# Seven half products with sums of halves for layer 1's scores, in place of eight

## The chip, the core and the metric

The program runs on one core of a Trainium2 chip. The metric is the device time of one execution in microseconds (us); the time of a kernel is the median of its runs. Engines are named as in the profile: PE (TensorE matmuls), PEld (TensorE weight loads), DVE (VectorE), ACT (ScalarE), POOL (GpSimd) and SP (SyncE, here an issuer of DMAs).

## The reference, cut to what matters

The input is 8 images of 256 channels and 32 x 32 positions, all in fp32. Layer 0 is attention with 8 heads. Layer 1 works on the tokens `t` (8 batches, 1024 tokens, 256 channels):

```python
t = t + attn(_ln_t(t), W)          # layer 1, attention
t = t + ffn(_ln_t(t), ...)         # layer 1, top 2 of 8 experts
...
xa = jnp.einsum('bnd,ed->bne', x, W)
scores = jnp.einsum('bne,bme->bnm', xa, x)
attn = jax.nn.softmax(scores, axis=-1)
y = jnp.einsum('bnm,bmd->bnd', attn, x)
```

The scores of a batch are a product of a 1024 x 256 matrix (`xa`) and a 256 x 1024 matrix (the normed tokens, turned). The softmax runs along each row, and its weights multiply the normed tokens.

## The kernel before, in words

One loop runs over the eight batches. In each, `layer0` computes layer 0's attention, `attend` layer 1's attention, and `normed` and `dispatch` the second norm, the gates of the experts and the scattering of tokens to them. Experts are worked for batches 0 to 6 together (`experts`) between layer 0 and `attend` of the last batch, and the last batch goes through all experts (`dense`). The results of the seven others are added up during `attend` and `dense` of the last batch, at the places where `tick` is called (class `Results`).

Engines take their instructions in the order in which they stand in that engine's queue. A scheduler has set that order from dependences and priorities; `issue_after` adds an edge for it alone. Work of the next batch is put in at the places where `attend` and `normed` call `fill`: class `Begin` issues the next batch's value products (`pv`, L399) and first projections (`pqk`, L340) there.

`attend` (L661 to L758) works on tiles of 128 tokens, so a batch has NT = 8 blocks. It normalises the tokens (`n1`), turns them to channels in `nT` (two halves of 128 channels, 1024 tokens each), and multiplies by W to get `xa` (`px`, L673, evicted by DVE at L680). For each block i, `scores(i)` makes four products of 128 x 512 (L688: two channel halves accumulate, for two halves of the tokens), DVE takes the maximum of the 1024 scores (L696), and ACT makes the exponentials with their sum (L699). The weights have then to be turned. For blocks 1 to 6, `turn` does it by a DVE transpose of squares of 32 (L706, into `sq`) and 16 moves of squares (L713, into `aT`), half by ACT copies and half by DMAs that SP issues. For blocks 0 and 7, `turn_now` uses TensorE transposes (L720) and one DVE copy (L722). `mix` multiplies the turned weights with the normed tokens (eight products of 128 x 256, L729), and DVE divides by the sum and adds the residual (L735). A block's mix stands two blocks behind its scores.

Exponentials, squares and turned weights come from one pool of six tiles (`expp`), which is also the pool of layer 0's exponentials (L520), and are taken in turn. PSUM has three tiles of two banks (`big`) and two of one bank (`acc`). The tiles of `two` named `qk0` and `qk1` hold layer 0's queries and keys, and in the last batch the hidden rows of `dense` and the results to store. The single tile `res` of `one` holds layer 0's result until its last product (L654), and in the last batch alternates with `v` as the home of the other batches' sums (`Results.load`).

Of the kernel before, what the change touches and what calls it, by code (L numbers as in the profile page):

```python
# [10 lines left out]
F32 = mybir.dt.float32  # L11
I32 = mybir.dt.int32
AF = mybir.ActivationFunctionType
# [6 lines left out]
def kernel(  # L20
# [49 lines left out]
    one = ctx.enter_context(tc.tile_pool(name="one", bufs=1))  # L70
    two = ctx.enter_context(tc.tile_pool(name="two", bufs=2))
    four = ctx.enter_context(tc.tile_pool(name="four", bufs=4))
    expp = ctx.enter_context(tc.tile_pool(name="expp", bufs=6))
    small = ctx.enter_context(tc.tile_pool(name="small", bufs=6))
    rowp = ctx.enter_context(tc.tile_pool(name="rowp", bufs=4))
    keep = ctx.enter_context(tc.tile_pool(name="keep", bufs=8))
    ps_big = ctx.enter_context(tc.tile_pool(name="ps_big", bufs=3, space=bass.MemoryType.PSUM))
    ps_acc = ctx.enter_context(tc.tile_pool(name="ps_acc", bufs=2, space=bass.MemoryType.PSUM))

    def big(name):  # L80

        return ps_big.tile([P, 1024], F32, tag="big", name=name)

    def acc(name):

        return ps_acc.tile([P, 512], F32, tag="acc", name=name)
# [146 lines left out]
    class Norm:  # L233


        def __init__(self, t, dst, eps, name):
            self.t, self.dst, self.eps, self.name = t, dst, eps, name
            self.mv = small.tile([P, NT, 2], F32, tag="mv", name=f"mv_{name}")
            self.rstd = small.tile([P, NT], F32, tag="rstd", name=f"rstd_{name}")
# [213 lines left out]
    def layer0(b, xT, begun, routing, xs):  # L453
# [61 lines left out]
        def soften(at, h):  # L515

            g, j = steps[at]
            if h == 0:
                sums[at] = small.tile([P, 2], F32, tag="sums", name=f"sums_{b}_{g}_{j}")
            ex = expp.tile([P, 1024], F32, tag="exps", name=f"ex_{b}_{g}_{j}_{h}")  # L520
            nc.scalar.activation(  # L521
                ex,
                pss.pop((at, h)),
                AF.Exp,
                bias=nmaxes.pop((at, h)),
                scale=1.0,
                accum_out=sums[at][:, h : h + 1],
            )
            exps[at, h] = ex
# [129 lines left out]


    def attend(b, t1, fill, tick=nothing):  # L661
        n1 = one.tile([P, NT, D], F32, tag="n", name=f"n1_{b}")
        layer_norm(t1, n1, 1e-5, f"a{b}")
        fill("norm 1")
        nT = one.tile([P, NCC, S], F32, tag="nT", name=f"nT_{b}")
        to_channels(n1, nT, f"n1_{b}")
        fill("normed 1")
        xa = one.tile([P, NCC, S], F32, tag="xa", name=f"xa_{b}")
        for ec in range(NCC):
            px = big(f"px_{b}_{ec}")  # L670
            for dc in range(NCC):
                for n in range(NH2):
                    nc.tensor.matmul(  # L673
                        px[:, ts(n, 512)],
                        WT[:, dc, ts(ec, P)],
                        nT[:, dc, ts(n, 512)],
                        start=(dc == 0),
                        stop=(dc == NCC - 1),
                    )
            tick(("xa", ec), nc.vector.tensor_copy(xa[:, ec, :], px))  # L680

        t2 = t1

        def scores(i):
            psc = big(f"ps1_{b}_{i}")
            for ec in range(NCC):
                for n in range(NH2):
                    nc.tensor.matmul(  # L688
                        psc[:, ts(n, 512)],
                        xa[:, ec, ts(i, P)],  # L690
                        nT[:, ec, ts(n, 512)],
                        start=(ec == 0),
                        stop=(ec == NCC - 1),
                    )
            nmax = small.tile([P, 1], F32, tag="nmax", name=f"nmax_{b}_{i}")
            tick(("max", i), nc.vector.tensor_reduce(nmax, psc, AX.X, ALU.max, negate=True))  # L696
            ex = expp.tile([P, 1024], F32, tag="exps", name=f"ex1_{b}_{i}")
            ssum = small.tile([P, 1], F32, tag="ssum", name=f"ssum_{b}_{i}")
            nc.scalar.activation(ex, psc, AF.Exp, bias=nmax, scale=1.0, accum_out=ssum)  # L699
            return ex, ssum  # L700

        def turn(i, ex):


            sq = expp.tile([P, S], F32, tag="exps", name=f"sq_{b}_{i}")
            nc.vector.transpose(sq, ex)  # L706
            aT = expp.tile([P, S], F32, tag="exps", name=f"aT_{b}_{i}")
            to = aT.rearrange("p (m a q) -> p a m q", a=NQ, q=SQ)
            since = sq.rearrange("p (m k q) -> p k m q", k=NQ, q=SQ)
            for a in range(NQ):  # L710
                for k in range(NQ):
                    move = nc.sync.dma_start if (a + k) % 2 else nc.scalar.copy
                    move(to[ts(k, SQ), a], since[ts(a, SQ), k])  # L713
            return [aT[:, ts(m, P)] for m in range(NT)]

        def turn_now(i, ex):

            pt = big(f"pa_{b}_{i}")
            for m in range(NT):
                nc.tensor.transpose(pt[:, ts(m, P)], ex[:, ts(m, P)], ident)  # L720
            aT = two.tile([P, S], F32, tag="tr", name=f"aT_{b}_{i}")
            nc.vector.tensor_copy(aT, pt)  # L722
            return [aT[:, ts(m, P)] for m in range(NT)]

        def mix(i, aT, ssum):
            ahead = fill("last products") if i == NT - 1 else None
            py = acc(f"py_{b}_{i}")
            for m in range(NT):
                nc.tensor.matmul(  # L729
                    py[:, :D], aT[m], n1[:, m, :], start=(m == 0), stop=(m == NT - 1)  # L730
                )
            rs = small.tile([P, 1], F32, tag="rs1", name=f"rs1_{b}_{i}")
            nc.vector.reciprocal(rs, ssum)
            with tc.issue_after(ahead.ins) if ahead else nullcontext():
                mixed = nc.vector.scalar_tensor_tensor(  # L735
                    t2[:, i, :], py[:, :D], rs, t1[:, i, :], ALU.mult, ALU.add
                )
            tick(("mixed", i), mixed)

        pending = []
        for i in range(NT):
            ex, ssum = scores(i)
            if 0 < i < NT - 1:
                ex = turn(i, ex)
            pending.append((i, ex, ssum))
            if i == 2:
                first, ex, ssum = pending.pop(0)
                mix(first, turn_now(first, ex), ssum)  # L750
            elif i > 2:
                mix(*pending.pop(0))
        fill("last weights")
        (last, ex, ssum) = pending.pop()
        ex = turn_now(last, ex)
        mix(*pending.pop())
        mix(last, ex, ssum)
        return t2  # L758


# [423 lines left out]
    class Results:  # L1184
# [67 lines left out]
        def add(self):  # L1252
            at = self.added
            if at == len(self.units):
                return
            assert at < self.sent
            self.added += 1
            b, i = self.units[at]
            n = at // NT
            gate = self.group.kept[b][0]  # L1260
            total = self.totals[n]
            for k in range(2):
                added = nc.vector.scalar_tensor_tensor(
                    total[:, i, :],
                    self.slot(at)[:, k, :],
                    gate[:, k, i : i + 1],
                    total[:, i, :],
                    ALU.mult,
                    ALU.add,
                )  # L1270
# [10 lines left out]
        def tick(self, place, behind=None):  # L1281
            added, sent, stored = self.PLACES.get(place, (0, 0, 0))
            if place == ("max", 0):
                self.scored = behind
            if added:
                with tc.issue_after(behind.ins):
                    for _ in range(added):
                        self.add()
            for _ in range(sent):
                self.gather(behind)  # L1290
            for _ in range(stored):
                if self.whole:
                    b, total, n = self.whole.pop(0)
                    store(b, total, n)
# [135 lines left out]
    for b in range(B):  # L1430
# [71 lines left out]
```

## Time and profile before

| what | value |
|---|---|
| median of 3 runs | 2321.36 us (2319.68 to 2324.47) |
| profiled execution, its own time | 2336.53 us |
| its span | 2333.8 us |
| mean granted TensorE clock | 0.992 |
| PE, L688 (scores of layer 1) | 228.5 us in 512 records |
| PE, L729 (mix of layer 1) | 234.3 us in 1024 records |
| ACT, L713 (turning copies) | 154.4 us in 384 copies |
| DVE, L696 (maxima) | 77.9 us in 64 |
| ACT, L699 (exponentials) | 71.3 us in 64 |

A row of the profile's groups has the line, the engine, the operation, output and inputs by the program's names, the shapes, the count, then the busy time in us and the mean of one in ns, and behind the second bar the idle time of the engine just before these instructions, with what ended most of it. An fp32 matmul leaves two records, so that 32 products a batch over eight batches are the 512 records of L688. The chain of waits is followed back from the last instruction; each piece of it is either work or a wait. The table of stretches gives, for each stretch, the busy time of every engine and the number of its instructions.

### The profile page before, as it was taken

The numbers are of one execution on the slowest core, as the hardware profiler recorded it, in microseconds if no ns is written. First come the engines' busy times: TensorE is split into PE (matmuls) and PEld (weight loads), VectorE is DVE, ScalarE is ACT, GpSimd is POOL, SyncE is SP. The second block draws the span as 40 slices with busy tenths as digits, with TensorE's granted clock in tenths as the row PEclk, the third lists the DMA queues.
The fourth block names the chain that finished last, engine by engine and source line by source line (L and its number), as shares of the span: only waits on it lengthen the run. The fifth ranks groups of instructions, "written<-read, shape, count | busy, mean of one in ns | idle before, by whom it ended". The sixth has DMA issues, their size and how long they took to land.

```text
span 2333.8 us, 37688 instructions
## 1 busy us (share of the span) xinstructions
PE 2276.1 (98%) x13123; PEld 1230.4 (53%) x13123; DVE 1528.1 (65%) x3757; ACT 1093.0 (47%) x1955; POOL 409.7 (18%) x392
## 2 busy tenths in 40 slices
PE   9999999999999999999999999999998999999698
PEld 3345534663456335633564356435643388886465
DVE  5775578557855785578657764777568756435755
ACT  3663466346634663556355645465545622223211
POOL 0000012000200020003000300020002134445563
PEclk9999999999999999999999999999999999999899
DMA  8995201020102010201020102000110247765574
GB/s 294 385 386 153 67 14 42 10 55 11 46 5 59 6 51 1 46 19 53 3 46 19 49 8 46 19 26 12 27 38 19 78 110 192 196 188 170 160 211 111
DMA packets 278756, 200.07 MB, mean 86 GB/s; under 512 B 189576, under 2 KB 232232, under 8 KB 276776
## 3 DMA queue, kind: packets, MB, share of 16 engines
q1 hardware_dynamic: 252472, 139.14, 21.2%
q0 software_dynamic: 25008, 58.01, 7.8%
q8 instruction: 104, 1.70, 0.3%
q10 hardware_dynamic: 1088, 0.52, 0.1%
q14 instruction: 84, 0.69, 0.1%
HBM read 108.88 MB, written 110.90 MB: 94 GB/s over the span
## 4 chain that ended last, share of the span: by engine, by line
PE 88%; DVE 4%; DMA 3%; issue 3%; ACT 1%; POOL 0%; another core or an unknown queue 0%; SPq 0%; DVEq 0%; ACTq 0%; POOLq 0%
PE po L557 19%; PE psc L480 18%; PE ps L688 9%; PE py L729 8%; PE pqk L362 7%; PE pr L654 5%; PE pv L399 4%; PE ph L1119 3%; PE pe L1145 3%; PE pdy L1392 3%; PE pdh L1368 2%; PE px L673 2%; PE pqk L340 2%; DMA y<-yb 1%; DVE n L254 1%
## 5 line engine op out<-in xcount | busy, mean ns | idle before, releaser
L521 ACT ACTIVATE ex<-psc,nmax 128x1024 f32<-128x1024 f32 x512 | 570.0, 1114 | 308.9 <-DVE scrap L504 222.9
L557 PE MATMUL po<-ex,vs 64*64 64x512 f32 x4096 | 569.3, 592 | 9.9 <-SPq L567 9.0
L480 PE MATMUL psc<-qk,qk 64*64 64x512 f32 x4096 | 574.1, 593 | 3.4 <-ACT ex L521 3.3
L504 DVE TENSOR_SCALAR_CACHE_REDUCE scrap<-psc,nmax 128x512 f32<-128x512 f32 x512 | 384.5, 751 | 163.4 <-PE psc L480 136.2
L495 DVE TENSOR_REDUCE nmax<-psc 128x1 f32<-128x512 f32 x512 | 350.8, 685 | 9.5 <-PE psc L480 9.5
L480 PEld LDWEIGHTS psc<-qk,qk 64*64 64x64 f32 x4096 | 179.1, 132 | 280.1 <-ACT ex L521 131.5
L557 PEld LDWEIGHTS po<-ex,vs 64*64 64x64 f32 x4096 | 173.9, 132 | 285.6 <-issue 84.3
L729 PE MATMUL py<-n,aT 128*128 128x256 f32 x1024 | 234.3, 383 | 4.4 <-DMA aT<-sq 4.4
L688 PE MATMUL ps<-nT,xa 128*128 128x512 f32 x512 | 228.5, 592 | 0.0
L729 PEld LDWEIGHTS py<-n,aT 128*128 128x128 f32 x1024 | 196.3, 192 | 54.8 <-issue 27.2
L933 POOL DMA_INDIRECT rows<-n,d_at x112 | 108.8, 972 | 661.2 <-DVE nmax L495 660.9
L713 ACT COPY aT<-sq 32x256 f32<-32x256 f32 x384 | 154.4, 402 | 80.0 <-DVE sq L706 52.4
L860 POOL TENSOR_TENSOR t<-t,n 128x2048 f32<-128x2048 f32 x8 | 36.3, 4533 | 878.2 <-DVE n L254 878.2
L362 PE MATMUL pqk<-xT,wqkv 128*128 128x512 f32 x384 | 171.2, 599 | 0.0
L688 PEld LDWEIGHTS ps<-nT,xa 128*128 128x128 f32 x512 | 96.6, 190 | 102.4 <-issue 95.1
L696 DVE TENSOR_REDUCE nmax<-ps 128x1 f32<-128x1024 f32 x64 | 77.9, 1217 | 84.9 <-PE ps L688 84.9
L327 ACT ACTIVATE qk<-pqk,b_qks 128x512 f32<-128x512 f32 x124 | 85.6, 690 | 94.2 <-PE pqk L362 77.1
L362 PEld LDWEIGHTS pqk<-xT,wqkv 128*128 128x128 f32 x384 | 71.0, 190 | 99.9 <-issue 76.8
L1241 POOL DMA_INDIRECT yk<-y,yat x112 | 110.2, 984 | 73.7 <-issue 34.0
L399 PE MATMUL pv<-wqkv,xT 128*128 128x512 f32 x256 | 120.6, 599 | 1.5 <-DVE v L407 1.0
L654 PE MATMUL pr<-wo,res 128*128 128x256 f32 x512 | 111.9, 379 | 0.0
L654 PEld LDWEIGHTS pr<-wo,res 128*128 128x128 f32 x512 | 97.2, 190 | 17.0 <-ACT res L576 3.2
(209 smaller groups left out, 2333.7 us busy)
## 6 DMA issues: line engine op xcount, KB each, us to landing
rows<-wb SPq DMA_DIRECT2D x7, 8192.0 KB
xr<-rows SPq DMA_DIRECT2D x252, 64.0 KB
y<-yb POOLq DMA_DIRECT2D x63, 256.0 KB
aT<-sq SPq DMA_DIRECT2D x384, 32.0 KB
xs<-in_x_dram SPq DMA_DIRECT2D x64, 128.0 KB
out_dram<-oT SPq DMA_DIRECT2D x60, 128.0 KB
xT<-in_x_dram SPq DMA_DIRECT2D x7, 1024.0 KB
sums<-t SPq DMA_DIRECT2D x7, 1024.0 KB
```

The lines of the kernel that those rows point to most:

```text
L362: mm = nc.tensor.matmul(pq[:, ts(n, 512)], wqkv[:, cc, t, ts(g, P)], xT[:, cc, ts(n, 512)], start=(cc == 0), stop=(cc == NCC - 1),)
L399: nc.tensor.matmul(pv, self.xT[:, cc, ts(i, P)], wqkv[:, cc, 2, :], start=(cc == 0), stop=(cc == NCC - 1),)
L480: mm = nc.tensor.matmul(pss[at, h][ts(c, DK), ts(n, 512)], k[r, j * P + c * DK : j * P + (c + 1) * DK], q[r, ts(n, 512)], start=True, stop ...
L495: firsts[at, h] = nc.vector.tensor_reduce(nmax, pss[at, h][:, ts(0, 512)], AX.X, ALU.max, negate=True)
L504: seconds[h] = nc.vector.tensor_scalar(scrap, pss[at, h][:, ts(1, 512)], -1.0, nmaxes[at, h], ALU.mult, ALU.min, accum_out=nmax,)
L521: nc.scalar.activation(ex, pss.pop((at, h)), AF.Exp, bias=nmaxes.pop((at, h)), scale=1.0, accum_out=sums[at][:, h : h + 1],)
L557: mm = nc.tensor.matmul(po[n][ts(h, DK), :], vss[at][keys, h, :], exps[at, h][keys, ts(n, 512)], start=(j == 0 and turn == 0), stop=(j == ...
L654: nc.tensor.matmul(pr[:, :C], res[:, g, ts(i, P)], wo[:, g, :], start=(g == 0), stop=(g == NPAIR - 1))
L688: nc.tensor.matmul(psc[:, ts(n, 512)], xa[:, ec, ts(i, P)], nT[:, ec, ts(n, 512)], start=(ec == 0), stop=(ec == NCC - 1),)
L713: move(to[ts(k, SQ), a], since[ts(a, SQ), k])
L729: nc.tensor.matmul(py[:, :D], aT[m], n1[:, m, :], start=(m == 0), stop=(m == NT - 1))
L1241: ins = nc.gpsimd.indirect_dma_start(out=self.slot(at)[:, k, :], out_offset=None, in_=self.group.y[:, :], in_offset=bass.IndirectOffsetOnAxis(
```

## The change

The score product of a batch is taken as a product of 2 x 2 matrices of halves: `xa` in halves of tokens (rows) and channels, the normed tokens in halves of channels and tokens. In place of eight half products it makes seven, in the form that shares sums (Winograd's form of Strassen's product). For this, four sums of halves of `nT` (t1 to t4) and four of `xa` (s1 to s4, of which one takes the place of a quarter of `xa`) are made by DVE; the quarters of `xa` that stay are copied by ACT. The sums lie in `res`.

The blocks go in pairs: pair k holds block k and block k + 4, and the mixes come in the order 0, 4, 1, 5, 2, 6, 3, 7. A pair has seven products of 128 x 512 (L750 of the new program) in three banks: `x` and the second bank of one `big` tile, and `z`, an `acc` tile. The product in `x` is accumulated four times; three times on the way ACT copies it into the tile of the exponentials. DVE adds what lies in the other banks to these copies in a fused instruction that also negates and keeps the running minimum (`tensor_tensor_reduce`). Exponentials of the second block of a pair are made in two halves, one from PSUM and one from the tile. The tiles of exponentials, squares and turned weights are no longer taken in turn but fixed by a table (`EX`, `SQ_AT`), with two more tiles from `qk0` and `qk1` (in the last batch both from `qk0`). The turning itself is as before, except that two of the blocks have their moves ordered behind a copy of a later pair.

```diff
-    expp = ctx.enter_context(tc.tile_pool(name="expp", bufs=6))
+    expp = ctx.enter_context(tc.tile_pool(name="expp", bufs=1))
...
+        EX = [6, 0, 1, 2, 4, 5, 2, 3]
+        SQ_AT = {1: (3, None), 2: (0, 7), 3: (1, 6), 4: (0, 1), 5: (4, 7), 6: (5, 6)}
...
+        xa = one.tile([P, NCC, NH2, HALF], F32, tag="xa", name=f"xa_{b}")
+        mixes = one.tile([P, 7, HALF], F32, tag="res", name=f"mixes_{b}")
+        b11, b12, b21, b22 = (nT[:, e, ts(n, HALF)] for e in range(2) for n in range(2))
+        t1_, t2_, t3_, t4_ = (mixes[:, i, :] for i in range(4))
+        nc.vector.tensor_sub(t1_, b12, b11)
+        nc.vector.tensor_sub(t2_, b22, t1_)
+        nc.vector.tensor_sub(t3_, b22, b12)
+        nc.vector.tensor_sub(t4_, b21, t2_)
+        a11, s3_, a12, a22 = (xa[:, e, n, :] for e in range(2) for n in range(2))
+        s1_, s2_, s4_ = (mixes[:, 4 + i, :] for i in range(3))
...
-            tick(("xa", ec), nc.vector.tensor_copy(xa[:, ec, :], px))
+            pxs.append(px)
+            if ec == 0:
+                nc.scalar.copy(a11, px[:, :HALF])
+                tick(("xa", ec), nc.vector.tensor_sub(s3_, a11, px[:, HALF:]))
+            else:
+                nc.scalar.copy(a22, px[:, HALF:])
+                nc.scalar.copy(a12, px[:, :HALF])
+                nc.vector.tensor_add(s1_, a22, pxs[0][:, HALF:])
+                nc.vector.tensor_sub(s2_, s1_, a11)
+                tick(("xa", ec), nc.vector.tensor_sub(s4_, a12, s2_))
...
+                self.product(self.x, a11, b11, True)
+                one_ = nc.scalar.copy(left, self.x)
+                second = self.product(v, a12, b21, True)
+                tc.declare_no_dep(second.ins, one_.ins, reason="the other bank")
+                self.product(self.x, s2_, t2_, False)
+                self.second = nc.scalar.copy(right, self.x)
+                self.product(self.z, s1_, t1_, True)
+                self.product(self.x, s3_, t3_, False)
+                nc.scalar.copy(far, self.x)
+                self.add(left, v, 3.0e38, self.low[0])
+                self.add(far, self.z, 3.0e38, self.low[1])
...
+            def rest(self):
+                k = self.k
+                self.product(self.z, s4_, b22, False)
+                self.product(self.x, a22, t4_, False)
...
+                tick(("max", 2 * k), self.add(ex0[:, HALF:], self.z, self.low[0], nmax[0]))
+                nc.scalar.activation(
+                    ex0, ex0, AF.Exp, bias=nmax[0], scale=-1.0, accum_out=ssum[0][:, 0:1]
+                )
+                last = nc.vector.tensor_scalar(
+                    scrap, self.x, -1.0, self.low[1], ALU.mult, ALU.min, accum_out=nmax[1]
+                )
...
+        pairs = [Pair(0), Pair(1)]
+        first, second = pairs[0].rest()
+        second = turned(*second)
+        third, fourth = pairs[1].rest()
+        third = turned(*third)
+        now = turn_now(0, first[1])
+        pairs.append(Pair(2))
+        fourth = turned(*fourth, pairs[2].second)
+        mix(0, now, *first[2:])
+        mix(*second)
+        fifth, sixth = pairs[2].rest()
+        fifth = turned(*fifth)
+        mix(*third)
+        pairs.append(Pair(3))
+        sixth = turned(*sixth, pairs[3].second)
+        mix(*fourth)
+        seventh, eighth = pairs[3].rest()
+        seventh = turned(*seventh)
+        mix(*fifth)
         fill("last weights")
...
+        mix(*sixth)
+        now = turn_now(7, eighth[1])
+        mix(*seventh)
+        mix(7, now, *eighth[2:])
```

More of the change, by code (lines that the diff above doesn't have):

```diff
@@ L78, with exp_tile @@
     ps_acc = ctx.enter_context(tc.tile_pool(name="ps_acc", bufs=2, space=bass.MemoryType.PSUM))
+    NEXP = 6
+    exp_turn = [0]
+    def exp_tile(name, at=None):
+        if at is None:
+            at = exp_turn[0] % NEXP
+            exp_turn[0] += 1
+        return expp.tile([P, 1024], F32, tag=f"exps{at}", name=name)
     def big(name):
@@ L519, in soften @@
                 sums[at] = small.tile([P, 2], F32, tag="sums", name=f"sums_{b}_{g}_{j}")
-            ex = expp.tile([P, 1024], F32, tag="exps", name=f"ex_{b}_{g}_{j}_{h}")
+            ex = exp_tile(f"ex_{b}_{g}_{j}_{h}")
             nc.scalar.activation(
@@ L661, in attend @@
     def attend(b, t1, fill, tick=nothing):
+        spare = [
+            two.tile([P, S], F32, tag="qk0" if b == B - 1 else f"qk{i}", name=f"spare_{b}_{i}")
+            for i in range(2)
+        ]
+        homes = [exp_tile(f"home_{b}_{i}", i) for i in range(NEXP)] + spare
+        EX = [6, 0, 1, 2, 4, 5, 2, 3]
+        SQ_AT = {1: (3, None), 2: (0, 7), 3: (1, 6), 4: (0, 1), 5: (4, 7), 6: (5, 6)}
         n1 = one.tile([P, NT, D], F32, tag="n", name=f"n1_{b}")
@@ L667, in attend @@
         fill("normed 1")
-        xa = one.tile([P, NCC, S], F32, tag="xa", name=f"xa_{b}")
+        HALF = S // 2
+        xa = one.tile([P, NCC, NH2, HALF], F32, tag="xa", name=f"xa_{b}")
[8 more added lines that the diff above has]
+        s1_, s2_, s4_ = (mixes[:, 4 + i, :] for i in range(3))
+        pxs = []
         for ec in range(NCC):
@@ L679, in attend @@
                     )
-            tick(("xa", ec), nc.vector.tensor_copy(xa[:, ec, :], px))
-        t2 = t1
[L684 to L700, printed above, removed]
@@ L702, in turn @@
-        def turn(i, ex):
-            sq = expp.tile([P, S], F32, tag="exps", name=f"sq_{b}_{i}")
+            pxs.append(px)
[8 more added lines that the diff above has]
+                tick(("xa", ec), nc.vector.tensor_sub(s4_, a12, s2_))
@@ new lines, in attend, with __init__, product, add @@
+        t2 = t1
+        NK = NT // 2
+        BLOCKS = [k + NK * h for k in range(NK) for h in range(2)]
+        class Pair:
+            def __init__(self, k):
+                self.k = k
+                both = big(f"ps1_{b}_{k}")
+                self.x, v = both[:, :HALF], both[:, HALF:]
+                self.z = acc(f"ps1z_{b}_{k}")
+                self.ex = [homes[EX[2 * k + h]] for h in range(2)]
+                self.low = [
+                    small.tile([P, 1], F32, tag=f"nlow{h}", name=f"nlow_{b}_{k}_{h}")
+                    for h in range(2)
+                ]
+                left, right = (self.ex[0][:, ts(n, HALF)] for n in range(2))
+                far = self.ex[1][:, ts(1, HALF)]
+                at = ts(k, P)
+                self.product(self.x, a11, b11, True)
[9 more added lines that the diff above has]
+                self.add(far, self.z, 3.0e38, self.low[1])
+            def product(self, to, stationary, moving, start):
+                return nc.tensor.matmul(
+                    to,
+                    stationary[:, ts(self.k, P)],
+                    moving,
+                    start=start,
+                    stop=True,
+                    skip_group_check=not start,
+                )
+            def add(self, dst, psum, low, to):
+                return nc.vector.tensor_tensor_reduce(
+                    out=dst,
+                    in0=dst,
+                    in1=psum,
+                    scale=-1.0,
+                    scalar=low,
+                    op0=ALU.add,
+                    op1=ALU.min,
+                    accum_out=to,
+                )
[3 more added lines that the diff above has]
+                self.product(self.x, a22, t4_, False)
+                nmax, ssum = [], []
+                for h in range(2):
+                    nmax.append(small.tile([P, 1], F32, tag="nmax", name=f"nmax_{b}_{2 * k + h}"))
+                    ssum.append(small.tile([P, 2], F32, tag="ssum", name=f"ssum_{b}_{2 * k + h}"))
+                ex0, ex1 = self.ex
+                tick(("max", 2 * k), self.add(ex0[:, HALF:], self.z, self.low[0], nmax[0]))
+                nc.scalar.activation(
+                    ex0, ex0, AF.Exp, bias=nmax[0], scale=-1.0, accum_out=ssum[0][:, 0:1]
+                )
+                last = nc.vector.tensor_scalar(
+                    scrap, self.x, -1.0, self.low[1], ALU.mult, ALU.min, accum_out=nmax[1]
+                )
+                tick(("max", 2 * k + 1), last)
+                nc.scalar.activation(
+                    ex1[:, :HALF],
+                    self.x,
+                    AF.Exp,
+                    bias=nmax[1],
+                    scale=1.0,
+                    accum_out=ssum[1][:, 0:1],
+                )
+                nc.scalar.activation(
+                    ex1[:, HALF:],
+                    ex1[:, HALF:],
+                    AF.Exp,
+                    bias=nmax[1],
+                    scale=-1.0,
+                    accum_out=ssum[1][:, 1:2],
+                )
+                return [(2 * k, ex0, ssum[0][:, 0:1], None), (2 * k + 1, ex1, *self.halves(ssum[1]))]
+            def halves(self, ssum):
+                return ssum[:, 0:1], ssum[:, 1:2]
@@ L706, in turn @@
+        def turn(i, ex, behind):
+            at_sq, at_aT = SQ_AT[i]
+            sq = homes[at_sq]
             nc.vector.transpose(sq, ex)
-            aT = expp.tile([P, S], F32, tag="exps", name=f"aT_{b}_{i}")
+            if at_aT is None:
+                aT = two.tile([P, S], F32, tag="tr", name=f"aT_{b}_{i}")
+            else:
+                aT = homes[at_aT]
             to = aT.rearrange("p (m a q) -> p a m q", a=NQ, q=SQ)
@@ L712, in turn @@
                     move = nc.sync.dma_start if (a + k) % 2 else nc.scalar.copy
-                    move(to[ts(k, SQ), a], since[ts(a, SQ), k])
+                    with tc.issue_after(behind.ins) if behind else nullcontext():
+                        move(to[ts(k, SQ), a], since[ts(a, SQ), k])
             return [aT[:, ts(m, P)] for m in range(NT)]
@@ L723, in turn_now, with mix @@
             return [aT[:, ts(m, P)] for m in range(NT)]
-        def mix(i, aT, ssum):
-            ahead = fill("last products") if i == NT - 1 else None
+        def mix(at, aT, ssum, more):
+            i = BLOCKS[at]
+            ahead = fill("last products") if at == NT - 1 else None
             py = acc(f"py_{b}_{i}")
@@ L732, in mix @@
             rs = small.tile([P, 1], F32, tag="rs1", name=f"rs1_{b}_{i}")
+            if more is not None:
+                nc.vector.tensor_add(rs, ssum, more)
+                ssum = rs
             nc.vector.reciprocal(rs, ssum)
@@ L737, in mix, with turned @@
                 )
[L738 to L752, printed above, removed]
+            tick(("mixed", at), mixed)
+        def turned(at, ex, ssum, more, behind=None):
+            return at, turn(at, ex, behind), ssum, more
+        pairs = [Pair(0), Pair(1)]
[17 more added lines that the diff above has]
+        mix(*fifth)
         fill("last weights")
[L754 to L757, printed above, removed]
+        mix(*sixth)
+        now = turn_now(7, eighth[1])
+        mix(*seventh)
+        mix(7, now, *eighth[2:])
         return t2
```

## The prediction

> **What bounds the kernel now.** I read the page first: the shares of busy time, then the chain of work that ended last.
>
> ```profile
> PE 2276.1 (98%) x13123; PEld 1230.4 (53%) x13123; DVE 1528.1 (65%) x3757; ACT 1093.0 (47%) x1955; POOL 409.7 (18%) x392
> ...
> PE 88%; DVE 4%; DMA 3%; issue 3%; ACT 1%; POOL 0%; another core or an unknown queue 0%; SPq 0%; DVEq 0%; ACTq 0%; POOLq 0%
> ```
>
> TensorE is busy nearly always and owns 88% of the chain, so matmul time removed is a gain only if TensorE then finds its next operands ready. That is a question for one stage, so I asked for the busy time of a middle batch (batch 1) from its first px matmul to its last py matmul, and from there to the logits:
>
> ```profile
> 436.26:503.41 67.15, 67.15 (x234) 42.69 (x233) 31.77 (x51) 31.50 (x66) 0.00 (x0) 1.00 0.24 40
> 503.41:511.95 8.54, 8.54 (x32) 4.39 (x31) 7.19 (x16) 1.58 (x3) 3.50 (x1) 1.00 0.01 2
> ```
>
> The columns are stretch, length, then PE, PEld, DVE, ACT and POOL. TensorE is busy for the whole 67.15 us and the whole 8.54 us: no stall to recover. DVE (31.77) and ACT (31.50) are half full. The chain over the end of this stretch says what stands between the last py and the logits:
>
> ```profile
> 503.41 3.43 PE pqk L340 x8
> 506.84 1.72 PE pv L399 x4
> 508.56 1.75 PE pt_n L272 x16
> 510.30 1.72 PE pv L399 x4
> ```
>
> The next batch's projection and values hide the layer norm that DVE makes in that time. Last, how ACT's work is cut (groups with their shapes; the number after the comma is the mean in ns):
>
> ```profile
> L713 ACT COPY aT<-sq 32x256 f32<-32x256 f32 x384 | 154.4, 402 | 80.0 <-DVE sq L706 52.4 <-DVE rs L733 19.7 <-issue 4.1
> L699 ACT ACTIVATE ex<-ps,nmax 128x1024 f32<-128x1024 f32 x64 | 71.3, 1113 | 55.4 <-DVE nmax L696 43.7 <-DVE rs L733 6.7 <-issue 4.5
> L576 ACT COPY res<-po 128x512 f32<-128x512 f32 x64 | 34.3, 587 | 30.9 <-PE po L557 30.9
> L504 DVE TENSOR_SCALAR_CACHE_REDUCE scrap<-psc,nmax 128x512 f32<-128x512 f32 x512 | 384.5, 751 | 163.4 <-PE psc L480 136.2
> ```
>
> A turned block puts eight copies of 0.40 us on ACT in one piece (3.31 us at a spacing of 0.414).
>
> [...] ACT's eight copies of one block always run as one piece. [...] 689 ns for L407 with one operand in PSUM, so I price each half sum at 0.69. [...] (the pairs of L1377 start 0.585 us apart at 0.683 each, the pairs of copies at L576 0.47 apart at 0.587). [...]
>
> **The change part by part.** Scores of one batch were 8 blocks of 4 products; they become 4 pairs of 7. A product is two records and takes 0.859 us (eight records in 3.43 us in the chain). Removed: 4 x 0.859 = 3.43 us of TensorE a batch, 27.5 us over eight.
>
> Added, a batch: on DVE seven half sums (0.69 each, 0.61 apart), 12 fused adds with a running minimum, 4 half maxima; away go 8 full maxima of 1.22 and two copies of xa. On ACT 3 copies of px, 12 copies of 0.587 out of PSUM, and 8 exponentials of which 4 are cut in halves: a full one holds ACT for 1.10 (its accumulator read starts at 1.01 and lets the next start 0.09 later), a half one 0.68 (less 512 elements at 0.826 ns, from 1113 ns for 1024 and L327's 690 ns for 512). Unchanged: 48 turning copies, 48 DMAs a batch on SP (0.66 apart, the eight landed 6.7 us after the transpose; the consumers come later than that).
>
> The unknown is the fused add. I take the nearest row, TENSOR_SCALAR_CACHE_REDUCE at 0.751, spaced 0.68. Bounds: 0.65, since it cannot beat the plain add by more than noise, to 1.37, an add and a reduce in a row (0.69 + 0.68).
>
> Now I lay the built order of the three queues against these durations. Time 0 is the first px matmul; a matmul that waited starts 0.25 us after its release (behind xa's copy, done at 444.40, the weight load starts at 444.44, takes 0.19, and the matmul follows).
>
> (a) px ends at 6.87, one product needs only a11 and runs. The second needs the copy of a12, behind that of a22 on ACT: released 8.14, starts 8.39. Stall 0.63. Half sums s1, s2, s4 on DVE are done at 8.4, 9.1, 9.9, just in time; t1 to t4 lie beside px.
>
> (b) Each accumulation on x must be copied out before the next: matmul, ACT copy, matmul. The order weaves pairs 0 and 1, which covers most; 0.18 + 0.18 + 0.12, and 0.18 in pair 2, stay: 0.66.
>
> (c) The third copies of the two pairs end at 13.7 and 17.3; DVE's adds wait for them, so the first maximum is there at 19.5. Then ACT is never idle: exponentials 1.10 + 0.68 + 0.68 + 1.10 + 0.68, eight turning copies 3.31, half an exponential 0.68, eight more copies 3.31: 11.54, until 31.05. Only then comes pair 2's first copy, and TensorE needs it: 31.63, product at 31.88. TensorE had run out at 30.3. Stall 1.56. In the same burst pair 3's first product waits for block 5's exponential to free its bank (0.54) and py of block 0 for its copy on DVE (0.24).
>
> (d) From there to the last py nothing waits: copies, adds and DMAs are ahead. But the four pqk products that stood behind the last py are now ordered ahead of it. Work to the last py: 67.15 - 3.43 + 3.43 = 67.15, plus stalls 0.63 + 0.66 + 0.54 + 0.24 + 1.56 = 3.63: 70.8.
>
> (e) Behind it 5.2 us of TensorE work are left to cover the norm (1.72 + 1.76 + 1.72). DVE: t 0.48, statistics 0.43 + 0.18, rstd, then the values' add of 0.69 that stands in its queue ahead of the reciprocal, and only then eight normalisations at 0.32. The first transpose starts 3.4 after the last py where TensorE is free at 1.7: stall 1.66, with 0.13 and 0.48 for the last rows and the copy of nT: 2.27. Logits at 70.8 + 7.5 = 78.2; before, 75.7. Net +2.5 us a batch, since 5.9 of stalls outweigh 3.43. Layer 0 of the next batch follows on the same queue and gives nothing back.
>
> Seven batches: +17.5. In the last, others' results are added on DVE and stalls exist already (4.41 on a DMA, 7.30 before pa). DVE's added work there is 3.8 us (16 x 0.68 and 7 x 0.61 against 10 x 1.14), and o_2's load now waits on SP for the buffer of the half sums, with a turned block's DMAs behind it. 0 if the gathers set the pace, 13 if both add up; I take 6. Sum +23.5, on the profiled execution's own 2336.53 us: 2360. The median of the runs is 0.65% under that execution; 2321.36 x 2360/2336.53 = 2345.
>
> **The rivals.** One: TensorE stays the bound. If the copies and adds keep ahead, 27.5 us less work shows in full: 2336.53 - 27.5, in the median 2294. For it speaks that ACT and DVE are half empty; against it the burst in (c), which is a matter of order, not of load. It decides from stalls under 3.4 us a batch. 0.10. Two: the burst hides (ACT's copies come when needed) but the tail stays: -3.43 + 0.63 + 0.66 + 2.27 = +0.1 a batch, 2322. 0.08. Three: the fused add is slow. Three stand in a row before the first exponential and two before each later one; 1.1 us costs 2 us a batch more, 2363; 1.37 some 4, 2377. 0.17. My forecast: 0.65.
>
> **How the numbers follow.** The range goes from 2318 (rival two with its noise) to 2376 (rival three); rival one, and a little above, is left out. 0.2% of this time is 4.6 us, about what the measurement can tell from none: faster 0.10, same 0.08, slower 0.82.
>
> **What would show it.** Idle time of TensorE before the score products, released by ACT copies, some 2 us a batch around pair 2; idle time before pt_n released by DVE's n; px to logits near 78 us in a middle batch with TensorE busy 72.3 of it; the fused add near 0.75. It is wrong if px to logits takes under 75.7, or if the fused add is far from 0.75.

## The result, and the profile after

| kernel | median | runs |
|---|---|---|
| before | 2322.68 us | 2319.68 to 2324.47 (6 runs) |
| after | 2350.14 us | 2344.68 to 2352.72 (6 runs) |
| ratio | 1.0117 | 95% interval 1.0103 to 1.0131 |

The changed kernel is slower by 27.5 us; 2345 had been forecast, in a range of 2318 to 2376. Its profiled execution took 2352.09 us for a span of 2350.1. The page's line of busy times and its shares of the chain, of the kernel after:

```profile
PE 2270.4 (97%) x13059; PEld 1213.5 (52%) x13059; DVE 1560.2 (66%) x4029; ACT 1165.0 (50%) x2139; POOL 412.1 (18%) x392
...
PE 82%; ACT 5%; DVE 5%; DMA 4%; issue 3%; SPq 0%; POOL 0%; DVEq 0%; ACTq 0%; POOLq 0%
```

TensorE's share of the chain fell from 88% to 82%, and ACT, which had 1%, now has 5%. TensorE's busy time fell by only 5.7 us, where 27.5 us of matmuls were taken away; the end of a matmul's record lies beyond the start of the next one (a product of two records counts 1.02 us, and the next starts after 0.86), so that a part of every pause counts as busy, and the first record after a pause counts 0.70 us in place of 0.59. Some small matmuls were also cut into groups that take longer (shown below). The middle batch says more. In the lines that follow, `pt_n` are the transposes of the normed tokens, `pl` the products for the logits of the gates, and `psc` the score products of layer 0. The stretches of batch 1 in the kernel after: from the first px to the end of the last py, from there to the logits, and from there to the next values (columns as in the prediction):

```profile
438.14:508.40 70.26, 68.35 (x234) 42.07 (x233) 35.91 (x85) 41.80 (x91) 0.00 (x0) 1.00 0.23 38
508.40:515.54 7.14, 5.67 (x26) 2.88 (x24) 6.02 (x16) 0.21 (x1) 1.26 (x1) 1.00 0.00 1
515.54:519.44 3.90, 3.90 (x28) 0.98 (x28) 2.33 (x3) 0.37 (x1) 3.26 (x1) 1.00 0.02 4
```

Before, TensorE was busy for all of the first two stretches. Now it is short of 1.9 us in the first and 1.5 in the second. ACT has gone from 31.50 to 41.80 us in the first stretch; in batch 2 it works from 700.00 to 712.71 with no pause above 0.05. Counted from the first px matmul (436.10 before, 438.14 after), the matmul behind the last py starts at 67.14 before and 70.26 after, the logits start at 75.85 and 77.40, and the values behind them at 78.72 and 81.39. The same three numbers come in every middle batch to 0.02 us. From px to px a batch takes 242.84 us in place of 240.12: +2.72.

The waits of TensorE in a middle batch (batch 2), read off the starts of its records one by one (what lies between two starts beyond the usual spacing), are 0.57 before the second product, two of 0.08 in the chains on x, 0.51 before pair 3's first product, 0.15 at block 0's mix, 1.62 and 0.08 in pair 2, and 1.51 + 0.29 behind the last py: 4.90 in all, where 3.43 us of work was saved. The largest is in TensorE's timeline (start, busy, then in brackets the idle time before it and what ended it). Between the two starts lie 2.38 us, 1.52 more than the 0.86 of a product, and 0.10 follows in the first record behind the pause; the bracket shows less, since it counts from the end of the record:

```profile
709.89 1.02 PE L408 MATMUL pv<-wqkv,xT 128*128 128x512 f32 x2
712.27 1.98 PE L750 MATMUL ps<-mixes 128*128 128x512 f32 x4 [1.36 <-ACT home L738]
```

and ACT's timeline of the same kernel says why that copy came so late:

```profile
704.31 3.28 ACT L825 COPY aT<-home 32x256 f32<-32x256 f32 x8
707.61 0.72 ACT L796 ACTIVATE home<-home,nmax 128x512 f32<-128x512 f32 x1
708.24 0.18 ACT L796 ACTIVATION_READ_ACCUMULATOR home<-home,nmax 128x1 f32 x1
708.33 3.28 ACT L825 COPY spare<-home 32x256 f32<-32x256 f32 x8
711.64 1.07 ACT L738 COPY home<-ps 128x512 f32<-128x512 f32 x2
```

The products to be copied were there before 706.3 (the last of them start at 704.47); the two copies wait until 711.64 because two turned blocks stand ahead of them.

### The profile page after: what moved, and what is told of

Its sections match the earlier page's. It is cut to its first block, busy times and chain, and to the rows that moved or that the text cites. A ratio compares the mean times of both kernels' runs of the same rounds, so it can differ in the third digit from the quotient of the medians.

```text
span 2350.1 us, 37998 instructions
## 1 busy us (share of the span) xinstructions
PE 2270.4 (97%) x13059; PEld 1213.5 (52%) x13059; DVE 1560.2 (66%) x4029; ACT 1165.0 (50%) x2139; POOL 412.1 (18%) x392
## 4 chain that ended last, share of the span: by engine, by line
PE 82%; ACT 5%; DVE 5%; DMA 4%; issue 3%; SPq 0%; POOL 0%; DVEq 0%; ACTq 0%; POOLq 0%
PE po L566 18%; PE psc L489 18%; PE py L842 7%; PE pqk L371 7%; PE pr L663 5%; PE ps L750 4%; PE pv L408 4%; PE ph L1246 3%; PE pe L1272 3%; PE pdh L1495 2%; PE px L700 2%; PE pdy L1519 2%; PE pqk L349 2%; PE ps1z L750 1%; DMA y<-yb 1%
## 5 line engine op out<-in xcount | busy, mean ns | idle before, releaser
L489 PE MATMUL psc<-qk,qk 64*64 64x512 f32 x4096 | 580.3, 593 | 3.6 <-ACT ex L530 3.5
L842 PE MATMUL py<-n,spare 128*128 128x256 f32 x512 | 117.3, 383 | 5.8 <-DMA out_dram<-oT 3.8
L842 PEld LDWEIGHTS py<-n,spare 128*128 128x128 f32 x512 | 98.2, 192 | 32.7 <-issue 20.0
L825 ACT COPY spare<-home 32x256 f32<-32x256 f32 x256 | 102.9, 402 | 3.2
L1256 ACT ACTIVATE hb<-ph,wb 128x256 f32<-128x256 f32 x96 | 40.4, 471 | 125.7 <-issue 86.6
L530 ACT ACTIVATION_READ_ACCUMULATOR ex<-psc,nmax 128x1 f32 x512 | 99.0, 193 | 0.0
L1246 PE MATMUL ph<-xb,wb 128*128 128x256 f32 x384 | 91.8, 381 | 6.3 <-DMA wb<-wpack,w_at 4.7
```

The lines of the kernel that those rows point to most:

```text
L489: mm = nc.tensor.matmul(pss[at, h][ts(c, DK), ts(n, 512)], k[r, j * P + c * DK : j * P + (c + 1) * DK], q[r, ts(n, 512)], start=True, stop ...
L530: nc.scalar.activation(ex, pss.pop((at, h)), AF.Exp, bias=nmaxes.pop((at, h)), scale=1.0, accum_out=sums[at][:, h : h + 1],)
L842: nc.tensor.matmul(py[:, :D], aT[m], n1[:, m, :], start=(m == 0), stop=(m == NT - 1))
L1246: last = nc.tensor.matmul(ph[:, ts(fc, BR)], wb[:, dc * FF + fc * P : dc * FF + (fc + 1) * P], xb[:, dc, :], start=(dc == 0), stop=(dc == ...
```

## The experiments

The chips differ by about 1% in the time of the kernel before (2340 to 2347 us there, 2322.7 in the first comparison), so times are read as ratios to the kernel before on the same chip. For single steps the middle batches are the sharper measure: in the kernels before and after, the times from px to the logits repeat to 0.02 us, on both chips. Where pqk is put back behind the last py (three of the runs below) they vary by 0.7 to 1.0 us, and a mean over batches 1 to 5 is given.

**The same two kernels on another chip.** No edit.

> The changed kernel once more, beside the kernel before on the chip of the experiments, since the last batch takes 214 us in its profile and 232 to 234 in those of the four edits. If that part is set by the chip, it shows 232 to 234 here too and the ratio to the kernel before stays at 1.012; if the edits lengthened it, 214 and again 1.012.

> The kernel before, profiled once more. Its first profiled execution lay 14 us over its timed runs and had 223 us in the last batch; if that was an accident of that execution, a second one has 209 to 214 there; if the last batch depends on the chip, 232 to 234 as in the four edits.

After: 2359.38 us, ratio 1.0084 (1.0069 to 1.0100); before 2342.04 in the profiled execution. The middle batches are the same as on the first chip (77.40 and 75.85 to the logits, 242.84 and 240.12 a batch). The rest isn't:

| part of the span (us) | before, first | after, first | before, again | after, again |
|---|---|---|---|---|
| batch 0, px to px | 246.62 | 248.71 | 246.61 | 247.03 |
| five middle batches | 1200.96 | 1214.59 | 1200.95 | 1214.62 |
| batch 6, the experts and layer 0 of batch 7 | 473.61 | 483.24 | 478.07 | 477.58 |
| last batch to the end | 223.13 | 214.09 | 225.09 | 229.36 |

(First px of each batch to the next; the last row to the end of the span.) The five middle batches cost 13.6 us more both times. The two last rows, where tokens are scattered and gathered by DMAs, gave +9.6 and -9.0 the first time, -0.5 and +4.3 the second. Neither expectation was met to the number: the ratio is 1.0084 and not 1.012, the last batch of the kernel after takes 229, between 214 and the 232 to 234 of the edits, and that of the kernel before 225, so its 223 was no accident. That part differs from one profiled execution to the next; one profile of each kernel on a chip cannot tell whether the chip or the execution sets it.

**The block order alone.** The kernel before, with:

```diff
+        BLOCKS = [k + NT // 2 * h for k in range(NT // 2) for h in range(2)]
...
-                        xa[:, ec, ts(i, P)],
+                        xa[:, ec, ts(BLOCKS[i], P)],
...
+        def mix(at, aT, ssum):
+            i = BLOCKS[at]
```

> The kernel before with its blocks of layer 1 scored and mixed in the order 0, 4, 1, 5, 2, 6, 3, 7 and nothing else: the same work in each place, so 1.000 within 0.2%. Rival: the order of the rows costs time by itself, in the layer norm behind the last block or in the last batch's gathers, and part of the changed kernel's 0.8% to 1.2% is found here.

Ratio 1.0004 (0.9995 to 1.0012), 75.85 us to the logits and 240.12 a batch. The order of the blocks costs nothing; the loss lies in the rest of the change.

**One copy moved ahead in ACT's queue.** The moves of block 1 are ordered behind pair 2's first copy:

```diff
-                one_ = nc.scalar.copy(left, self.x)
+                one_ = self.first = nc.scalar.copy(left, self.x)
...
-        third = turned(*third)
         now = turn_now(0, first[1])
         pairs.append(Pair(2))
+        third = turned(*third, pairs[2].first)
```

> The changed kernel, with ACT's second eight turning copies (block 1's) put behind pair 2's first copy instead of ahead of it; the work is the same. If order on ACT is what makes the 1.6 us stall before pair 2's second product on x (1.52 + 0.10 in the profile), the stall goes and seven or eight batches give 8 x 1.6 = 13 us back: about 2337. Rival, load: ACT and DVE have that work to do in that stretch anyway, so the wait reappears at a later copy or at block 1's py, and the time stays at 2350 (within 4).

Ratio 1.0117 (1.0098 to 1.0135), no better than the changed kernel's 1.0084 and 1.0117; 77.71 us to the logits against 77.40. TensorE's timeline of this kernel:

```profile
710.63 1.13 PE L750 MATMUL ps<-mixes 128*128 128x512 f32 x2 [0.18 <-ACT home L738]
711.59 1.03 PE L842 MATMUL py<-n,aT 128*128 128x256 f32 x4
713.06 1.12 PE L750 MATMUL ps<-mixes,xa 128*128 128x512 f32 x2 [0.45 <-ACT home L742]
```

The wait fell from 1.62 to 0.45 us, but 0.71 came up before the next product of the same pair (its copy at L742 stood behind five of the turning copies), and 0.73 before pair 3's third product, whose copy now has eight turning copies ahead of it. Together 1.89: the wait moved. That no order would help is not shown by it. ACT's timeline of this kernel shows that the copy moved ahead still stands behind the first eight turning copies and half an exponential, and the next copy behind five:

```profile
706.00 3.28 ACT L825 COPY aT<-home 32x256 f32<-32x256 f32 x8
...
710.01 0.56 ACT L738 COPY home<-ps 128x512 f32<-128x512 f32 x1
710.48 2.06 ACT L825 COPY spare<-home 32x256 f32<-32x256 f32 x5
712.44 0.57 ACT L742 COPY home<-ps 128x512 f32<-128x512 f32 x1
```

In the changed kernel the first eight turning copies are done at 707.6, while TensorE first uses their weights at 715.04, and ACT stands idle for 1.88 us once the burst is over:

```profile
715.04 3.62 PE L842 MATMUL py<-n,aT 128*128 128x256 f32 x16
720.34 1.15 ACT L781 ACTIVATE home<-home,nmax 128x1024 f32<-128x1024 f32 x1 [1.88 <-DVE nmax L760]
```

An order with all three copies of pair 2 ahead of both turned blocks might thus have found room. It was not tried, and whether the order or the load of ACT makes this wait stays open.

**The copies of pair 2 given to DVE.**

```diff
+                copy = nc.vector.tensor_copy if k in (2,) else nc.scalar.copy
-                one_ = nc.scalar.copy(left, self.x)
+                one_ = copy(left, self.x)
...
-                self.second = nc.scalar.copy(right, self.x)
+                self.second = copy(right, self.x)
...
-                nc.scalar.copy(far, self.x)
+                copy(far, self.x)
```

> The changed kernel, with the three copies of pair 2's products made by DVE instead of ACT: 3 x 0.587 less on ACT, about 3 x 0.65 more on DVE, which stands idle for 2.1 and 3.0 us in that stretch. If the stall before pair 2's second product is ACT's load between 700 and 712 us (not only its order, as moving the copy ahead changed nothing), it falls from 1.62 to under 0.4 us and comes back nowhere: 8 x 1.2 = 10 us less than the changed kernel, a ratio of 1.007. Rival: DVE is as full when it counts (three transposes and a copy stand in its queue until 708), and the stall keeps its size: 1.012.

Ratio 1.0033 (1.0021 to 1.0046); on the same chip the changed kernel has 1.0084. DVE's timeline of this kernel shows two of the copies, and a transpose between them:

```profile
701.67 0.65 DVE L739 COPY home<-ps 128x512 f32<-128x512 f32 x1
702.24 1.22 DVE L815 STREAM_TRANSPOSE home<-home 128x1024 f32<-128x1024 f32 x1
703.39 1.19 DVE L835 COPY aT<-pa 128x1024 f32<-128x1024 f32 x1
704.50 0.67 DVE L743 COPY home<-ps 128x512 f32<-128x512 f32 x1
```

No product of pair 2 on x waits for a copy any more; 0.27 us is left before a product on z. The logits come at 75.81, 1.59 earlier than in the changed kernel. The wait came from the queue on ACT that these copies shared with the turning copies, while DVE had room (it is busy for 35.91 of the 70.26 us of the changed kernel's first stretch). The edit takes work off ACT and the copies out of its queue at once, so it does not tell load from order either. A batch takes 241.3 us here, though, where the kernel before takes 240.12 with the same time to the logits. So 1.1 us a batch is lost behind the logits, which the next run explains.

**pqk back behind the last py.**

```diff
-            if place == "norm 1" or place == "norm 2":
+            if place == "norm 1":
...
+            if place == "norm 2":
+                with tc.issue_after(evicted["mixing"].ins):
+                    self.project(True)
...
-                nc.tensor.matmul(
+                evicted["mixing"] = nc.tensor.matmul(
```

The first two lines take the place out of the old condition; the last lets the edge start at the mix's last matmul.

> The changed kernel, with the next batch's four pqk products put back behind the last py, as in the kernel before. If the stalls behind the last py come from the norm's lost cover, TensorE's idle time before pt_n and pl (1.51 + 0.29 in the profile) goes, and with it the pair of psc products that stands alone between two halves of pl (about 1 us): 7 x 1.8 = 13 us to 7 x 2.8 = 19 us less, 2331 to 2337. Rival: the four products covered something where they stand now (block 5's and 7's turning), so that a wait of up to 3.4 us comes up before a late py and the time stays at 2350 or grows.

Ratio 0.9995 (0.9987 to 1.0004), level with the kernel before. The changed kernel's chain behind its last py has DVE on it:

```profile
751.41 1.73 PE pv L408 x4
...
753.16 0.69 DVE v L416
753.86 0.12 DVE rstd_f L261
...
754.00 0.42 DVE n L263
...
754.47 0.44 PE pt_n L281 x2
```

and its TensorE timeline goes on with the logits and layer 0's scores in pieces:

```profile
758.38 0.64 PE L895 MATMUL pl<-n2T,rT 128*32 128x256 f32 x8
758.95 1.07 PE L489 MATMUL psc<-qk,qk 64*64 64x512 f32 x2
759.95 0.64 PE L895 MATMUL pl<-n2T,rT 128*32 128x256 f32 x8
760.52 1.93 PE L489 MATMUL psc<-qk,qk 64*64 64x512 f32 x10
```

With pqk behind the last py, both are gone, as TensorE's timeline of that kernel shows:

```profile
743.55 1.88 PE L408 MATMUL pv<-wqkv,xT 128*128 128x512 f32 x4
745.27 1.91 PE L281 MATMUL pt_n<-ident,n 128*128 128x128 f32 x16
...
748.83 1.07 PE L898 MATMUL pl<-n2T,rT 128*32 128x256 f32 x16
749.83 1.93 PE L492 MATMUL psc<-qk,qk 64*64 64x512 f32 x12
```

The transposes start without a wait. The twelve psc records are six products, and they take 1.86 us from their start to the next matmul, as the ten records (five products) do in the changed kernel; the sixth product, put alone, costs 1.00 on top, and the logits in two pieces 0.14 (2 x 0.57 against 1.00): 1.14, about the 1.12 lost behind the logits (3.99 us from logits to values in place of 2.87). The five middle batches take 239.8 to 240.8 us, 240.3 in the mean, about the time of the kernel before (240.2). That this is so near is chance: 3.1 us of waits (the list above without those behind the last py) and a new one stand against 3.43 saved. The new one is the rival, in a small part: TensorE waits up to 1.0 us before the mix of the seventh block (the logits come at 75.55 to 76.50 us), where three of the four pqk products stood in the changed kernel (741.76 to 744.34 in batch 2).

**a12 copied ahead of a22 on ACT.**

```diff
-                nc.scalar.copy(a22, px[:, HALF:])
                 nc.scalar.copy(a12, px[:, :HALF])
+                nc.scalar.copy(a22, px[:, HALF:])
```

> The changed kernel, with the copy of a12 ahead of that of a22 on ACT. The stall of 0.57 us before the second product should go in each batch: 8 x 0.5 = 4 us, about 2346. Rival: s1 on DVE, which reads a22, comes 0.5 us later, and the fourth product waits for it or for s2 instead: no change (2350).

The wait of 0.57 fell to 0.08, and the logits come at 76.91, 0.49 earlier. Ratio 1.0066 (1.0051 to 1.0081): 0.2% and 0.5% under the changed kernel's two ratios (1.0084 and 1.0117). The middle batches explain 8 x 0.49 = 3.9 us, 0.17%; a difference beyond that is no larger than the one between those two ratios.

**The three edits together.**

> The three edits together: pair 2's copy ahead of the second eight turning copies, pqk behind the last py, a12 ahead of a22. If the stalls are independent they add up: 13 + 13 to 19 + 4 = 30 to 36 less, 2314 to 2320, a little under the kernel before (2323), since 3.43 us a batch less of matmul work then shows with some 1.3 us of smaller stalls left. Rival: the stalls are one another's cover (a stall that goes in one place comes back in the next), and the sum stays above 2330.

Ratio 1.0011 (1.0003 to 1.0018), between what the two theories gave. The middle batches take 239.7 to 240.2 us, 239.9 in the mean, 0.3 less than in the kernel before. The missing 13 us are those of the copy moved ahead: its waits (0.45, 0.71, 0.73) are here too. Against the changed kernel the mean is 3.0 us less; the single edits gave 0.45 (a12), 2.66 (pqk) and -0.22 (the copy), 2.9 together. So the stalls at px, in the burst and in the tail hardly cover one another.

**The two good edits with DVE's copies.** a12 first, pqk behind the last py, and pair 2's copies on DVE.

> pqk behind the last py, a12 ahead of a22, and pair 2's copies on DVE. The first two gave -0.5% to -1.2% each against the changed kernel; with 1.2 us a batch more from the third this should be 0.991 to 0.995 of the kernel before: the saved matmul time shows at last. Rival: the stretch has another limit (block 4's turned weights), and the time stays at 0.999.

2323.41 us where the kernel before has 2339.80: ratio 0.9930 (0.9916 to 0.9943), faster than both. Its stretches of batch 1, cut as before:

```profile
432.81:497.60 64.79, 64.54 (x226) 40.63 (x225) 37.45 (x88) 38.81 (x86) 0.00 (x0) 1.00 0.25 41
497.60:506.31 8.71, 8.71 (x34) 4.55 (x32) 7.19 (x16) 1.58 (x3) 3.50 (x1) 1.00 0.00 1
```

Its 64.79 us against 67.14 before: -3.43 of products and +1.0 of small waits. The second stretch is that of the kernel before (75.85 - 67.14 = 8.71), with TensorE busy throughout. The saved matmul time shows at last, at 1.8 to 2.4 us a batch, 2.2 in the mean; as with pqk put back alone, up to 0.7 us is lost before the mix of the seventh block.

**Every fused add twice.** Ahead of each fused add and minimum stands the same one into a scrap tile; nothing reads what it leaves there.

```diff
             def add(self, dst, psum, low, to):
+                again = small.tile([P, 1], F32, tag="again", name=f"again_{b}_{self.k}")
+                nc.vector.tensor_tensor_reduce(
+                    out=scrap,
...
+                    accum_out=again,
+                )
```

> The changed kernel with every fused add and minimum on DVE made twice (the first into a scrap tile): a block's add costs 1.37 instead of 0.68, the upper bound of the prediction's third rival, which priced it at 4 us a batch, 8 x 4 = 32 us: 1.4% over the changed kernel (1.008 to 1.012), 1.022 to 1.026. If DVE's slack takes it (DVE is busy 66% of the span), it stays within 0.3% of the changed kernel.

Ratio 1.0222 (1.0205 to 1.0238). A batch takes 247.0 us, 4.2 more than in the changed kernel, where 4 had been worked out. DVE has slack over the span (busy 66% of it in the changed kernel), but these adds stand in a row ahead of the exponentials.

## Why the prediction was right, step by step

The mechanism was right: fewer matmuls on a bound TensorE are a loss if ACT and DVE can't feed the rest in time (4.90 us of waits a batch here, against 3.43 of work saved). The signs and places of the waits were right; two sizes were off in opposite directions, and one part was not to be had by this working. That the median came within 5 us of the forecast is in part luck, as the last points say.

| step | forecast (us a batch) | measured |
|---|---|---|
| work removed | -3.43 | -3.43 (a product still takes 0.86) |
| (a) a12's copy behind a22's | 0.63 | 0.57 |
| (b) the chains on x | 0.66 | 0.25 |
| (c) pair 2's copy behind the burst | 1.56 | 1.62 |
| (c) pair 3's first product, block 0's mix | 0.54 + 0.24 | 0.51 + 0.15 |
| (e) behind the last py | 2.27 | 1.80 |
| px to logits | 75.7 to 78.2 | 75.85 to 77.40 |
| behind the logits | 0 | +1.12 |

- **The fused add.** 0.75 us was assumed, spaced 0.68, from the next-nearest row. The groups of the kernel after (columns as in the prediction):

```profile
L760 DVE CUSTOM_DVE_ANT_0 home<-home,ps1z 128x512 f32<-128x512 f32 x32 | 21.9, 683 | 0.0
L760 DVE CUSTOM_DVE_ANT_0 home<-home,ps1z,nlow 128x512 f32<-128x512 f32 x24 | 17.9, 746 | 7.9 <-PE ps1z L750 7.9
```

  It takes 0.683 to 0.688 with a fixed start value, as much as a plain add (0.687 for the values' add at L416), and 0.746 with one per row. Why the waits in (b) are 0.08 and not 0.12 to 0.18 was not worked out; no add stands in these chains. The upper bound of rival three was not met, but the price that the rival put on it was right, as the doubled adds showed. The half sums, priced at 0.69 after L407's 0.689, took 0.677 to 0.693 in the mean of a line. The working counted seven of them; there are eight (L689 to L692, L710, L714 to L716), 0.6 us more on DVE, and none of TensorE's waits in the list above ends with a half sum. By its own sum (2 us in eight batches) rival three's 2363 is 2361.
- **(c)** was right in size and place. Its words "a matter of order, not of load" are not decided: one copy moved ahead only moved the wait, and the copies on another engine took it away, but all copies of the pair ahead of the turning copies were not tried. The forecast took it that a copy on ACT waits out what stands ahead of it, and ACT's timelines of the two kernels show that: the copy at L738 starts at 711.64, just as the turning copies ahead of it end (708.33 + 3.28), and at 710.01 in the kernel with the copy moved, as half an exponential ahead of it ends (709.29 + 0.72).
- **(e)** was right in mechanism: the chain goes over the values' add and the reciprocal to n, as written, and pqk put back took it all away. The transposes started 3.22 us behind the last py, not 3.4. The sign "TensorE busy 72.3 of it" read 74.0 of 77.4 us, because a part of each pause counts as busy.
- **"Layer 0 of the next batch gives nothing back"** is the step that failed. Behind the logits 1.12 us a batch was lost, because pl was cut in two by a psc product; that came with pqk's new place, as the run that puts pqk back shows. It was missed since the working stopped at the logits. It made up for the 0.95 us too much on the way there: +2.5 a batch was forecast, +2.72 measured, and half of that agreement is luck.
- **Batch 0, the experts and the last batch.** +6 in the last batch was an estimate between 0 and 13. The profiles show -9.0 and +4.3 there, and +9.6 and -0.5 in the row with the experts. Whether the load of `o_2` behind the half sums' buffer delays a turned block's DMAs was not tried and stays open; differences of this size come from one profiled execution to the next (214 and 229 us for the last batch of the kernel after).
- **The scaling to the median.** The profiled executions differ by 15.6 us (2352.09 - 2336.53), the medians by 27.5. The forecast of +23.5 on the execution was 8 too high there, and 4 too low on the medians: the profiled execution of before was 14 us above its median, that of after only 2.

Of the rivals, the first (TensorE stays bound, 2294) was had only with the edits: with a12 first, DVE's copies and pqk back, about two thirds of the saving show in a middle batch. The second (burst hidden, tail stays) describes the kernel with DVE's copies and had priced it at 2322; it lies 0.33% above the kernel before because of the loss behind the logits.

## What to carry to other kernels

On an engine that is busy all the time, work removed is a gain only as far as its feeders keep up in that stretch (here 3.43 us a batch were removed and 4.90 waited): lay out the feeder's queue there from its first to its last instruction, and see what stands ahead of the short copy that is waited for. Moving the copies to an engine with room took the wait of 1.62 us away here; moving one copy ahead only shifted it (1.89 us in three waits). Matmuls that depend on nothing are the cover of a serial step; see what is left bare where they are moved away (here 1.80 us a batch behind the last py). Follow the built order past the point where the change ends, to where the next round starts.

## What was not expected of the hardware

- The fused add with a running minimum costs no more than a plain add of the same size (0.683 and 0.688 us at 128 x 512, where the plain add at L416 takes 0.687; 0.746 where the start value is one per row), and its read of the accumulator, 0.083 us, lies beside the next instruction.
- A product of 64 x 64 (two records) put alone between other matmuls costs 1.00 us, and nothing as the sixth of six (1.86 us for five and for six). In the trace of the kernel before, which has all six together too, the first records of four products start within 0.04 us (512.95 to 512.99) and those of the other two within 0.01 (513.86 and 513.87); in the changed kernel, the sixth and the one that was its neighbour each run alone (in batch 2 from 758.95 and from 761.43).
